# A recurrent stage in a kept order: swapped halves without state copies, gates split around tanh, sums and squares in place of bn_stats

## Chip, cores and metric

The kernel runs on one core of a Trainium2 chip. The metric is the device time of one execution in microseconds (us). The chip's engines are named as in the profile: PE is TensorE (PEld its weight loads), DVE is VectorE, ACT is ScalarE, POOL is GpSimd, and SP is SyncE, whose queue issues most of the DMAs.

## The reference, cut to what matters

Four layers work on x of shape (16, 32, 128, 128). Each adds to x a function of the group-normalised x (16 groups of two channels). The change lies in layer 0, a recurrence over the columns of a skewed image; the layers behind it are a quantised sum of absolute differences, a Hartley transform with mixing, and an encoder and decoder of convolutions.

```
xs[t] = W2 . skewed(norm(x))[:, :, :, t] + b2          # t = 0..127, (b, 4*32, h)
def step((pc, ph), xt):
    g  = xt + W1_prev . shift(ph) + W1_cur . ph + b1   # shift: by one row of h
    o, f, i = sigmoid(g[0:32]), sigmoid(g[32:64]), sigmoid(g[64:96])
    gg = tanh(g[96:128])
    nc = f * pc + i * gg
    nh = o * tanh(nc)
x1 = x + stack(nh over t)                              # then x1's mean and variance per group
```

All of it is float32. The mean and the variance of x1 are needed by the next layer before it can begin.

## The kernel before, in words

Partitions. The 512 rows of (batch, channel) form four groups g of 128 partitions, each of four batches by 32 channels. Stage 0 works on two chains c: chain 0 holds groups 0 and 1, chain 1 holds groups 2 and 3. A tile of a chain has 128 partitions and two column blocks, one per group.

Steps and chunks. The 128 time steps t are cut in NT = 16 chunks of T = 8. In chunk ch only the first n = min(8(ch+1)+2, 128) rows of h are computed, since the rows behind are equal to the last one; a tile of both groups has a width of 2n columns, 20 in the first chunk and 256 in the last. In each step the two chains take turns, so there are 256 chain steps, 16 in a chunk. At the end of a chunk the last column is spread to the rows that the next chunk adds (line 265).

The products. The weights are 64x64 blocks (two batches of 32 channels on the diagonal). A gate q needs three kinds of product: 0 with h, 1 with h shifted by one row, 2 with the normalised input xn. Each product is made of two matmuls on 64 partitions ("pair"), and each float32 matmul shows as two in the profile. For a gate with copy = 0 (F and G) input and output lie on the same half of the partitions. For a gate with copy = 1 (I and O) the weights of the other half of the array are used, so that four quadrants of the array work at once; these two gates read a copy of h with its halves swapped, the tile e (lines 258 to 260), and a copy of xn with its halves swapped, which SP makes by DMA after each normalise (line 177).

One chain step in the code (lines 223 to 265): sixteen products with h or e, eight products with xn for the next chain step, four gates on ACT (line 244: F, I, G, O, each reading a PSUM bank of its own), on DVE c*F (251), i*g (252) and their sum (253), tanh of c on ACT (255), h (256), and the two swapped copies into e (260).

Around the recurrence. `load(ch)` brings a chunk of xn and of the residual x (tile res) into SBUF. `normalise(ch, xn, g)` scales and shifts xn on ACT (line 174). `add` adds h to res on DVE (lines 185 and 188, the second for the rows beyond n), takes bn_stats of the result (189), and stores x1 (191). At the end bn_aggr (277) and norm_stats make the mean and the variance of x1.

The order. In stage 0 the order of the instructions on each engine is chosen by the scheduler of the framework. The function `keep_order(nc, tc, start)` makes every instruction since `start` follow the previous one of its engine in the order of the program; in the kernel before, only the stage behind (the differences, ACT and DVE bound) is kept that way. That stage and those after it are woven by a planner with costs of its own, which the change does not touch.

Of the kernel before, what the change touches and what calls it, by code (L numbers as in the profile page):

```python
# [100 lines left out]
def stage0(nc, tc, keep, cst, x, xs, w0, b1, b2, x1):  # L101
# [9 lines left out]
    PAIRS = ((F, I), (G, O))  # L111
    with ExitStack() as ctx:
# [33 lines left out]
        ex = [[sm.tile([128, 2, H + 1], F32, name=f"e_{c}_{i}") for i in range(2)] for c in range(2)]  # L146
        cs = [sm.tile([128, 2, H], F32, name=f"c_{c}") for c in range(2)]
        for c in range(2):
            nc.vector.memset(cs[c], 0.0)
            nc.vector.memset(hs[c][1][:, T - 1], 0.0)  # L150
            for i in range(2):
                nc.vector.memset(hs[c][i][:, :, :, 0], 0.0)
                nc.vector.memset(ex[c][i], 0.0)

        stat1 = sm.tile([128, NG, 32, 6], F32, name="stat1")
# [7 lines left out]
        def load(ch):  # L163
            steps = slice(T * ch * H, T * (ch + 1) * H)
            xn = [xp.tile([128, NG, T, H], F32, name=f"xn{i}") for i in range(2)]
            res = rp.tile([128, NG, T, H], F32, name="res")
            for g in range(NG):
                nc.sync.dma_start(flat(xn[0], g), bc_view(xs, g)[:, steps])
                nc.sync.dma_start(flat(res, g), bc_view(x, g)[:, steps])
            return xn, res  # L170

        def normalise(ch, xn, g):
            v = xn[0][:, g, :, : T * (ch + 1)]
            nc.scalar.activation(v, v, AF.Identity, bias=shift[:, g : g + 1], scale=r0[:, g : g + 1])
            for half in range(2):
                own, other = slice(64 * half, 64 * half + 64), slice(64 - 64 * half, 128 - 64 * half)
                nc.sync.dma_start(flat(xn[1], g)[own], flat(xn[0], g)[other])

        def add(ch, res, g, half):
# [4 lines left out]
            r = res[:, g, steps, :n]  # L184
            nc.vector.tensor_add(r, r, h[:, :, 1 : n + 1])
            if n < H:
                r = res[:, g, steps, n:]
                nc.vector.tensor_add(r, r, bcast(h[:, :, n], 2, H - n))
            nc.vector.bn_stats(stat1[:, g, 2 * ch + half, :], flat(res, g)[:, 512 * half : 512 * half + 512])
            if half:  # L190
                nc.sync.dma_start(bc_view(x1, g)[:, T * ch * H : T * (ch + 1) * H], flat(res, g))

# [5 lines left out]
        for g in range(NG):  # L198
            normalise(0, xn, g)

        with tc.tile_pool(name="s0_gps", bufs=1, space=PSUM) as gps:
            bank = [[gps.tile([128, 2, 256], F32, name=f"pg{c}_{q}") for q in range(4)] for c in range(2)]

            def product(c, kind, q, copy, pair, v, width):

                half = slice(64 * (pair ^ copy), 64 * (pair ^ copy) + 64)
                nc.tensor.matmul(  # L207
                    bank[c][q][64 * pair : 64 * pair + 64, :, :width],
                    wb[half, 4 * kind + KIND[q]].rearrange("p b o -> p (b o)"),
                    v[half],  # L210
                    start=kind == 2,
                    stop=kind == 1,
                    skip_group_check=True,
                )

            def inputs(c, t, xn):
                for gates in PAIRS:
                    for copy, q in enumerate(gates):
                        for pair in range(2):
                            v = xn[copy][:, 2 * c : 2 * c + 2, t % T, : t + 1]  # L220
                            product(c, 2, q, copy, pair, v, t + 1)

            inputs(0, 0, xn)
            for ch in range(NT):
                n = rows(ch)
                following = load(ch + 1) if ch + 1 < NT else None
                for j in range(T):
                    t = T * ch + j
                    for c in range(2):
                        h_in = (hs[c][ch % 2][:, j - 1] if j else hs[c][(ch - 1) % 2][:, T - 1], ex[c][t % 2])  # L230
                        h_out, cell = hs[c][ch % 2][:, j], cs[c][:, :, :n]
                        for gates in PAIRS:
                            for kind in range(2):
                                for copy, q in enumerate(gates):
                                    for pair in range(2):
                                        v = h_in[copy][:, :, 1 - kind : n + 1 - kind]
                                        product(c, kind, q, copy, pair, v, n)
                        if c == 0:
                            inputs(1, t, xn)
                        elif t + 1 < W:  # L240
                            inputs(0, t + 1, xn if j + 1 < T else following[0])
                        gt = gp.tile([128, 4, 2, H], F32, name=f"gt{c}")
                        for q in (F, I, G, O):
                            nc.scalar.activation(  # L244
                                gt[:, q, :, :n],
                                bank[c][q][:, :, :n],
                                AF.Tanh if q == G else AF.Sigmoid,
                                bias=bias[:, KIND[q] : KIND[q] + 1],
                            )
                        ig = gp.tile([128, 2, H], F32, name=f"ig{c}", bufs=1)  # L250
                        nc.vector.tensor_mul(cell, cell, gt[:, F, :, :n])
                        nc.vector.tensor_mul(ig[:, :, :n], gt[:, I, :, :n], gt[:, G, :, :n])
                        nc.vector.tensor_add(cell, cell, ig[:, :, :n])  # L253
                        th = gp.tile([128, 2, H], F32, name=f"th{c}")
                        nc.scalar.activation(th[:, :, :n], cell, AF.Tanh)  # L255
                        nc.vector.tensor_mul(h_out[:, :, 1 : n + 1], gt[:, O, :, :n], th[:, :, :n])  # L256
                        e_out = ex[c][(t + 1) % 2]
                        for half in range(2):
                            own, other = slice(64 * half, 64 * half + 64), slice(64 - 64 * half, 128 - 64 * half)
                            nc.vector.tensor_copy(e_out[own, :, 1 : n + 1], h_out[other, :, 1 : n + 1])  # L260
                        if j == T - 1 and n < H:

                            m = rows(ch + 1)
                            for v in (h_out[:, :, 1:], e_out[:, :, 1:], cs[c]):
                                nc.vector.tensor_copy(v[:, :, n:m], bcast(v[:, :, n - 1], 2, m - n))
                    if following and 2 <= j < 6:
                        normalise(ch + 1, following[0], j - 2)
                    if j >= T // 2:
                        add(ch, res, j - T // 2, 0)
                    elif ch:  # L270
                        add(ch - 1, previous, j, 1)
                previous = res
                if following:
                    xn, res = following
            for g in range(NG):
                add(NT - 1, previous, g, 1)
# [1702 lines left out]
```

## Time and profile before

| what | value |
|---|---|
| median of 3 runs | 7142.77 us (7139.5 to 7150.18) |
| the profiled execution, its own time | 7141.35 us |
| its span, first to last instruction | 7139.6 us |
| mean granted clock of TensorE | 0.907 |
| busy in the span: PE, DVE, ACT | 78%, 81%, 76% |
| first gate of stage 0; first h; last h | 96.8; 105.1; 841.4 us |
| ns_mean (statistics of x1 begin) | 846.9 us |

In the profile a row names a line of the kernel, the engine, the operation, the tile written and the tile read, the shapes and the count, then the busy time and the mean time of one. "Idle before" is the time for which the engine stood still just before these instructions, with what released it. The busy shares are means over stages that have different limits; those of the whole span say little about stage 0. In a timeline a row has the start, the duration, the engine and line, and instructions alike are merged in one row.

### The profile page before, as it was taken

The numbers are of one execution on the slowest core, as the hardware profiler recorded it, in microseconds if no ns is written. First come the engines' busy times: TensorE is split into PE (matmuls) and PEld (weight loads), VectorE is DVE, ScalarE is ACT, GpSimd is POOL, SyncE is SP. The second block draws the span as 40 slices with busy tenths as digits, with TensorE's granted clock in tenths as the row PEclk, the third lists the DMA queues.
The fourth block names the chain that finished last, engine by engine and source line by source line (L and its number), as shares of the span: only waits on it lengthen the run. The fifth ranks groups of instructions, "written<-read, shape, count | busy, mean of one in ns | idle before, by whom it ended". The sixth has DMA issues, their size and how long they took to land. (4 is left out here: it accounts for less than half of the span.)

```text
span 7139.6 us, 271100 instructions
## 1 busy us (share of the span) xinstructions
PE 5578.2 (78%) x127580; PEld 2940.1 (41%) x127580; DVE 5753.4 (81%) x7112; ACT 5452.3 (76%) x3099; POOL 81.9 (1%) x83
## 2 busy tenths in 40 slices
PE   4778667778876777999776787999886774698896
PEld 3666333333433333333333443333333343454564
DVE  7787689999998989999997999999998993134224
ACT  2555489999998989999998999999998991131222
POOL 0000000000000000000000001000000000000000
PEclk9899889999998999999888998999898996798997
DMA  8664211111123342221244243121243245252414
GB/s 312 225 211 147 83 62 58 60 59 39 56 88 108 121 107 87 62 78 37 70 121 114 96 135 112 52 76 50 66 106 120 68 133 166 80 173 73 98 40 99
DMA packets 372718, 722.55 MB, mean 101 GB/s; under 512 B 50896, under 2 KB 217296, under 8 KB 360720
## 3 DMA queue, kind: packets, MB, share of 16 engines
q1 hardware_dynamic: 364128, 670.79, 30.9%
q0 software_dynamic: 7040, 33.80, 1.4%
q8 instruction: 998, 16.35, 0.9%
q14 instruction: 120, 0.98, 0.0%
q10 hardware_dynamic: 432, 0.64, 0.0%
HBM read 507.28 MB, written 164.32 MB: 94 GB/s over the span
## 5 line engine op out<-in xcount | busy, mean ns | idle before, releaser
L705 ACT ACTIVATE d_act<-q,neg 128x8192 f16<-128x8192 f16 (+1 forms) x622 | 4402.5, 7149 | 182.1 <-PE acc L595 133.3
L708 DVE TENSOR_SCALAR d_dve<-q,qw 128x8192 f16<-128x8192 f16 (+1 forms) x1682 | 3877.5, 2361 | 168.0 <-PE acc L595 125.5
L595 PE MATMUL acc<-d_dve,sel 128*32 128x512 f16 x26912 | 1877.6, 403 | 507.3 <-DVE d_dve L708 441.5
L595 PEld LDWEIGHTS <-sel 128*32 128x32 f16 x36864 | 1022.7, 100 | 2203.4 <-issue 1547.7
L1670 PE MATMUL acc<-xp,wf 32*32 32x512 f32 x25600 | 1034.3, 616 | 44.0 <-issue 39.4
L595 PE MATMUL acc<-d_act,sel 128*32 128x512 f16 x9952 | 720.5, 411 | 376.1 <-ACT d_act L705 368.0
L1670 PEld LDWEIGHTS acc<-xp,wf 32*32 32x32 f32 x25600 | 420.5, 104 | 417.4 <-issue 329.8
L625 PE MATMUL acc<-q,zero 128*32 128x512 f16 x7088 | 510.1, 399 | 0.0
L1608 ACT ACTIVATE y<-pooled,b 32x128 f32<-32x128 f32 x488 | 195.0, 400 | 402.1 <-DVE pooled L1594 395.5
L207 PE MATMUL pg<-h,wb 64*64 64x20 f32 (+15 forms) x4096 | 397.6, 320 | 102.0 <-DVE h L256 60.7
L852 PE MATMUL acc<-y,u_conv 32*32 32x256 f32 (+1 forms) x9728 | 366.3, 474 | 76.5 <-issue 50.6
L244 ACT ACTIVATE gt<-pg,bias 128x20 f32<-128x20 f32 (+15 forms) x1024 | 314.9, 374 | 78.9 <-PE pg L207 71.7
L207 PE MATMUL pg<-e,wb 64*64 64x20 f32 (+15 forms) x4096 | 353.1, 315 | 18.2 <-DVE e L260 6.3
L1311 ACT ACTIVATE xp<-xp,shift,stats 128x1280 f32<-128x1280 f32 (+1 forms) x128 | 182.6, 1434 | 217.2 <-DMA xp<-x_d 193.6
L207 PEld LDWEIGHTS pg<-h,wb 64*64 64x64 f32 x4096 | 246.0, 153 | 137.5 <-DVE h L256 86.9
L625 PEld LDWEIGHTS <-zero 128*32 128x32 f16 x7088 | 215.0, 102 | 198.4 <-issue 44.7
L207 PE MATMUL pg<-xn,wb 64*64 64x28 f32 (+61 forms) x4096 | 283.6, 302 | 10.9 <-ACT gt L244 3.2
L207 PEld LDWEIGHTS pg<-e,wb 64*64 64x64 f32 x4096 | 250.1, 155 | 96.8 <-DVE e L260 67.6
L1352 PE MATMUL acc<-xp 32*64 32x204 f32 (+3 forms) x8576 | 242.3, 346 | 38.4 <-ACT xp L1317 28.6
L1799 DVE TENSOR_SCALAR s<-acc,l_ms,l_one 128x512 f32<-128x512 f32 x128 | 102.1, 820 | 207.1 <-PE acc L852 207.1
L255 ACT ACTIVATE th<-c 128x20 f32<-128x20 f32 (+15 forms) x256 | 81.3, 320 | 239.4 <-DVE c L253 238.0
L852 PEld LDWEIGHTS acc<-y,u_conv 32*32 32x32 f32 x9728 | 175.0, 112 | 196.8 <-issue 146.2
(215 smaller groups left out, 4070.5 us busy)
## 6 DMA issues: line engine op xcount, KB each, us to landing
xr<-x_d SPq DMA_DIRECT2D x192, 512.0 KB
xp<-x_d SPq DMA_DIRECT2D x112, 640.0 KB
q<-q_d SPq DMA_DIRECT2D x32, 2145.0 KB
x_d<-xr SPq DMA_DIRECT2D x128, 512.0 KB
x_in<-in_x_dram SPq DMA_DIRECT2D x16, 2048.0 KB
res<-in_x_dram SPq DMA_DIRECT2D x64, 512.0 KB
xn<-in_xs_dram SPq DMA_DIRECT2D x64, 512.0 KB
xn<-xn SPq DMA_DIRECT2D x128, 256.0 KB
```

The lines of the kernel that those rows point to most:

```text
L207: nc.tensor.matmul(bank[c][q][64 * pair : 64 * pair + 64, :, :width], wb[half, 4 * kind + KIND[q]].rearrange("p b o -> p (b o)"), v[half], ...
L244: nc.scalar.activation(gt[:, q, :, :n], bank[c][q][:, :, :n], AF.Tanh if q == G else AF.Sigmoid, bias=bias[:, KIND[q] : KIND[q] + 1],)
L595: self.nc.tensor.matmul(acc[k][32 * j : 32 * j + 32, :], self.sel16[:, i // 9, :], d[:, row : row + 4, c : c + W], start=first, stop=last,)
L625: self.nc.tensor.matmul(acc[k][32 * j : 32 * j + 32, :], self.zero, q[:, :4, :W], start=False, stop=False)
L705: nc.scalar.activation(dst, src, AF.Relu, bias=self.neg[:, i : i + 1])
L708: nc.vector.tensor_scalar(dst, src, self.qw[:, i : i + 1], 0.0, ALU.subtract, ALU.max)
L852: nc.tensor.matmul(acc[blk][32 * j : 32 * j + 32, o : o + rows * n], t[part, 4 * par + tap, :], src[part, top : top + rows, left : left + ...
L1311: nc.scalar.activation(v, v, AF.Identity, bias=self.shift3, scale=self.stats3[:, 1])
L1352: nc.tensor.matmul(gram[blk][j : j + width, at : at + n], xp[part, l, 2 + j : 2 + j + width], xp[part, rows, j : j + width + 4], start=sta ...
L1608: nc.scalar.activation(d, s, AF.Identity, bias=bj)
L1670: nc.tensor.matmul(acc[blk][32 * j : 32 * j + 32, :], tap_of("all", tap)[rows], xp[rows, 4 * j + kh : 4 * j + kh + 4, kw : kw + W], start= ...
L1799: nc.vector.tensor_scalar(s.rearrange("p r w b -> p b r w"), acc[blk].rearrange("p (b r w) -> p b r w", b=2, w=64), istd[:, blk : blk + 1] ...
```

## The change

- Gates I and G, in place of I and O, use the other half of the array (SWAPPED). They read the same h and xn as F and O, and their results come out on the swapped half of the partitions. The tile e, the copies into it, the second xn tile and its DMAs go.
- i*g is then made in two multiplies of 64 partitions that read the swapped half and write the own half.
- The chain step is written out in a fixed order, kept by `keep_order`: gates I and F, one piece of other ACT work (half a normalise, or a square), tanh of the chain step before, gates G and O. On DVE: one half of an add, h of the chain step before, c*F, i*g, c+i*g. The products run in the order I,F then G,O, and then the inputs of the next chain step.
- normalise works on four of the eight steps at a time.
- bn_stats and bn_aggr go. The add becomes a tensor_tensor_reduce that also sums its result; ACT squares the result less the mean of x (bias `away`) and sums the squares. Two reductions and four small operations make mean and variance from them.

```diff
-    PAIRS = ((F, I), (G, O))
+    SWAPPED = (I, G)
...
         def add(ch, res, g, half, part):
...
-            nc.vector.tensor_add(r, r, h[:, :, 1 : n + 1])
...
-            nc.vector.bn_stats(stat1[:, g, 2 * ch + half, :], flat(res, g)[:, 512 * half : 512 * half + 512])
+                nc.vector.tensor_tensor_reduce(
+                    r, r, v, 1.0, 0.0, ALU.add, ALU.add, accum_out=sums[:, g, ch, half, part : part + 1]
+                )
...
+        def square(ch, res, g, half):
+            nc.scalar.activation(
+                junk,
+                flat(res, g)[:, 512 * half : 512 * half + 512],
+                AF.Square,
+                bias=away[:, g : g + 1],
+                accum_out=squares[:, g, ch, half : half + 1],
+            )
...
+            def product(c, kind, q, v, width):
+                for pair in range(2):
+                    own = pair ^ (q in SWAPPED)
+                    half = slice(64 * own, 64 * own + 64)
+                    nc.tensor.matmul(
+                        bank[c][q][64 * pair : 64 * pair + 64, :, :width],
+                        wb[half, 4 * kind + KIND[q]].rearrange("p b o -> p (b o)"),
+                        v[half],
...
+            def state(c, ch, j, n, gt):
+                th = gp.tile([128, 2, H], F32, name=f"th{c}")
+                nc.scalar.activation(th[:, :, :n], cs[c][:, :, :n], AF.Tanh)
+                def write():
+                    h = hs[c][ch % 2][:, j]
+                    nc.vector.tensor_mul(h[:, :, 1 : n + 1], gt[:, O, :, :n], th[:, :, :n])
+                    if j == T - 1 and n < H:
+                        m = rows(ch + 1)
+                        for v in (h[:, :, 1:], cs[c]):
+                            nc.vector.tensor_copy(v[:, :, n:m], bcast(v[:, :, n - 1], 2, m - n))
+                return write
...
+                for s in range(2 * T):
+                    j, c = s // 2, s % 2
...
+                    for gates in ((I, F), (G, O)):
+                        for kind in range(2):
+                            for q in gates:
+                                product(c, kind, q, h_in[:, :, 1 - kind : n + 1 - kind], n)
+                    if c == 0:
+                        inputs(1, t, xn)
+                    elif t + 1 < W:
+                        inputs(0, t + 1, xn if j + 1 < T else following[0])
+                    gt = gp.tile([128, 4, 2, H], F32, name=f"gt{c}")
+                    gate(I)
+                    gate(F)
+                    if following and 3 <= s < 11:
+                        normalise(ch + 1, following[0], (s - 3) // 2, (s - 3) % 2)
+                    elif waiting:
+                        square(*waiting.pop(0))
+                    write = state(*before) if before else None
+                    if s >= T or ch:
+                        at = (ch, res, s // 2 - T // 2, 0) if s >= T else (ch - 1, previous, s // 2, 1)
+                        add(*at, s % 2)
+                        if s % 2:
+                            waiting.append(at)
+                    if write:
+                        write()
+                    gate(G)
+                    gate(O)
+                    nc.vector.tensor_mul(cell, cell, gt[:, F, :, :n])
+                    ig = gp.tile([128, 2, H], F32, name=f"ig{c}", bufs=1)
+                    for half in range(2):
+                        own, other = slice(64 * half, 64 * half + 64), slice(64 - 64 * half, 128 - 64 * half)
+                        nc.vector.tensor_mul(ig[own, :, :n], gt[other, I, :, :n], gt[other, G, :, :n])
+                    nc.vector.tensor_add(cell, cell, ig[:, :, :n])
+                    before = c, ch, j, n, gt
...
+            keep_order(nc, tc, start)
+            nc.vector.tensor_reduce(mv[:, :, 0], sums.rearrange("p g a b c -> p g (a b c)"), AX.X, ALU.add)
+            nc.vector.tensor_reduce(mv[:, :, 1], squares.rearrange("p g a b -> p g (a b)"), AX.X, ALU.add)
```

## The prediction

> **What bounds the kernel now.** I read the page first, then cut out the part that the change touches. The page gives one span and says nothing of stages:
>
> ```profile
> span 7139.6 us, 271100 instructions
> ```
>
> The recurrence runs from 96.8 us (first gate) to 841.4 us (last h), so 745 us of the 7139.6 can move. Everything behind it keeps its instructions and their order; it starts when the statistics of x1 are ready (ns_mean at 846.86 us) and moves with them. The groups of the window 100 to 845 us (line, engine, operation, tiles, count | busy us, mean ns | idle before it and its releasers):
>
> ```profile
> L244 ACT ACTIVATE gt<-pg,bias 128x20 f32<-128x20 f32 (+15 forms) x1022 | 314.4, 374 | 78.9 <-PE pg L207 71.7
> L260 DVE COPY e<-h 64x20 f32<-64x20 f32 (+15 forms) x512 | 117.2, 229 | 25.1 <-DVE h L256 0.5
> L189 DVE BATCH_NORM_STATS2 stat<-res 128x6 f32<-128x512 f32 x128 | 87.8, 686 | 0.7
> ```
>
> So 205 us of DVE go into state copies and bn_stats. Is DVE on the path? The waits of the same window (who waited for whom, us in total, times, longest):
>
> ```profile
> ACT th L255 <- DVE c L253: 238.0, 214, 5.3
> PEld pg L207 <- DVE h L256: 86.9, 110, 2.7
> DVE h L256 <- ACT th L255: 83.3, 188, 0.8
> ```
>
> ACT waits for DVE's cell in 214 of 256 steps, DVE for tanh in 188: the two hand one step to and fro. Timelines of one step at width 228 (columns of both batch groups together), ACT, then DVE, then PE:
>
> ```profile
> 717.11 0.39 ACT L255 ACTIVATE th<-c 128x228 f32<-128x228 f32 x1 [0.99 <-DVE c L253]
> 717.41 1.46 ACT L244 ACTIVATE gt<-pg,bias 128x228 f32<-128x228 f32 x4
> ```
> ```profile
> 717.54 0.40 DVE L256 TENSOR_TENSOR h<-gt,th 128x228 f32<-128x228 f32 x1 [0.52 <-ACT th L255]
> 718.04 0.56 DVE L260 COPY e<-h 64x228 f32<-64x228 f32 x2
> 718.63 0.40 DVE L251 TENSOR_TENSOR c<-c,gt 128x228 f32<-128x228 f32 x1
> 718.95 0.39 DVE L252 TENSOR_TENSOR ig<-gt 128x228 f32<-128x228 f32 x1
> 719.37 0.40 DVE L253 TENSOR_TENSOR c<-c,ig 128x228 f32<-128x228 f32 x1
> ```
> ```profile
> 718.90 0.36 PE L207 MATMUL pg<-e,wb 64*64 64x228 f32 x2
> ...
> 719.10 0.36 PE L207 MATMUL pg<-e,wb 64*64 64x228 f32 x2
> ...
> 719.29 0.36 PE L207 MATMUL pg<-e,wb 64*64 64x228 f32 x2
> ```
>
> One step is DVE's five pieces in a row plus the tanh that DVE waits for: 0.43 (tanh to h), 0.50, 0.60 (copies), 0.31, 0.42, 0.49 (sum to next tanh) = 2.75 us, the pace of the steady steps. PE needs 12 slots of 0.19 us (four quadrants at once): 2.3 us, no bound. The adds and bn_stats fall between chunks, where the pace is lost: at width 228 sixteen steps took 731.68 - 676.51 = 55.2 us, 3.45 each. From first h (105.13) to last (841.39): 736.3 / 255 = 2.89 us a step.
>
> **What the change makes of a step.** The kept order is, on ACT: I, F, one extra (half a normalise, or a square), tanh of the step before, G, O; on DVE: one add-with-sum, h of the step before, c*F, two halves of i*g, c+ig; on PE: I,F products (4 slots), G,O (4), inputs of the next step (4). The next PE step needs the h written in this one. So the loop becomes: tanh, h, I,F products, gates I and F, the extra, the next tanh. G, O and the cell update fall out of the loop, and the extra falls in. Its terms, from rows of before (W = width in columns):
> - tanh start to h start: 0.28 (W=52), 0.33 (116), 0.43 (228); h start to first matmul: 0.27, 0.34, 0.45.
> - I,F products to gate I: at 228 three slots 0.19, last matmul 0.36, first-use 0.05, and 0.06 from matmul end to gate (763.95 to 764.02 us): 1.04. At 116 (slot 0.10): 0.68. At 52 (slot 0.057): 0.50.
> - two gates: pitch 0.33 at 228 (1.46 us for four, last one 0.46), 0.24 at 116, 0.19 at 52: twice that.
> - the extra: a half normalise of N columns. The full one at N=512 starts 0.71 us before its follower, at N=256 0.49, so 0.28 + 0.00083 N. The square (512 columns, bias operand, summed) has no row. Lower end: the gates' pitch carried to 512, 0.57; upper: the normalise's 0.71 plus 0.1 for the sum, 0.8. I take 0.63: nearer the normalise without its second operand. 124 squares lie in the loop; the ends make -7 and +21 us.
> Sum: 1.01 + 0.00686 W + extra. By width, against the mean step of before:
>
> ```
> W       20    52    84    116   148   180   212   244   256
> before  2.62  2.52  2.42  2.55  2.75  3.07  3.34  3.56  3.5
> after   1.54  1.92  2.12  2.37  2.61  2.86  3.11  3.35  3.08
> ```
>
> (The first chunk has few extras, the last no normalise.) All sixteen widths, sixteen steps each: 648 us. The 15 chunk ends keep two of three boundary copies (0.17 us each, L265) ahead of a matmul: +7.5 us.
>
> **The clock, row against rule.** Between 120 and 125 us PE is busy 5.00 of 5.00 us, yet a weight load there takes 223 ns; at 345 us it takes 132 ns with PE busy only 3.54 of 5. The profile calls both granted clock 1.00. The Trainium skill ("TensorE: Matmul & The Clock Gate", Part 1) says some 4 us of sustained matmuls bring the full rate. By the rule the sum stays 655; by the row busy time is not enough at small widths, and the slow rate first ended near 205 us, at width 52, and came back in spells until about 300. I take the row: slots twice as long in the first five chunks, 0.28 to 0.33 us a step, 80 steps: +24 us, so 679 us for 256 steps, 676 for the 255 between first and last h.
>
> **DVE under it, and a rule against the change.** Added: one more multiply of 64 partitions (0.387 at 228) and a read of the accumulator in each add. The existing add-up of this kind shows the price (grouped by form):
>
> ```profile
> L1412 DVE CUSTOM_DVE_ANT_0 es_w<-acc,gm 128x420 f32<-128x420 f32 x80 | 47.5, 593 | 20.2 <-PE acc L1352 9.8 <-DMA gm<-in_gram_dram 7.2 <-DVE es_red L1412 0.5
> L1412 DVE DVE_READ_ACCUMULATOR2_ANT es_red<- 128x1 f32 x80 | 6.6, 82 | 0.0
> ```
>
> At 420 columns 593 ns, like a plain add (594 at 424), plus 82. Removed: two copies (0.56) and bn_stats (0.686 each, 128 times). In the trace independent DVE operations overlap by about 0.08 us (c*F at 718.63, 0.40 long, ig at 718.95). The skill ("VectorE: DVE Perf Modes", Two Vector instructions with no wait between them) says that one which starts in another quadrant than its forerunner is held until all earlier ones end. The halves of i*g cross partitions, so both are held, and the sum after them. With overlap DVE's step at 228, long add included, is 0.31 + 0.31 + 0.31 + 0.42 + 0.31 + 0.63 + 0.08 = 2.4 us, by the rule 2.7. Both are under the loop's 3.23, so I cost it at nothing; the cover is 0.5 us a step, and beyond it every 0.1 us costs 26 us. A late DVE would hold h, and behind it PE.
>
> **Queues.** SP loses 128 swap issues (0.46 to 2.15 us each, waiting for ACT) and 32 MB of traffic; PE waited 1.5 us for them once. The loads of xn no longer stand behind them. Eight loads of 512 KB need some 10 us at the 375 GB/s of a chunk's start; the first normalise stands at step 3, and SP issues the loads once the older xn is free, one step before the chunk: lead about 8 us for the first piece. An ACT wait there would stall tanh and both gates behind it; I cost it at nothing.
> Start: PE need not wait for the swapped input (matmuls on xn at 102.99 us after 1.51 us). Chain 1 still needs groups 2 and 3 (98.75 us), so I put the first h at 101.3 instead of 105.13. End: four adds (0.70 apart), one square, two reductions, four small operations: 5.9 us from last h to ns_mean, 5.5 before.
>
> **The sum.** 101.3 + 676.4 + 5.9 = 783.6 against 846.9: -63 us. Profiled execution: 7141.35, its span 7139.6, so 1.75 us lie around it. 7141.35 - 63 = 7078; the median of the runs is 1.4 above that execution: 7080.
>
> **Rivals.**
> - *The extra on ACT, or DVE, sits in the loop for more than I allow* (chance 0.18). Square at 0.8, held DVE operations that use up the cover at narrow widths (at W=36 the cover is only 0.2 us): 0.1 to 0.15 us a step, 25 to 38 us back: about 7112. For: four engines hand over in one loop and none of the small latencies has slack. Against: every latency is taken from the same tiles.
> - *The early chunks run at full clock* (0.10): -24 us, 7056. For: the products no longer wait in pairs, so matmuls come denser. Against: the row at 120 us.
> - *PE stays at half rate: slower* (0.07). PE now works 0.8 to 2.6 us of each step and pauses up to 1.2. If the gate never opens, 12 slots of W/600 us bind above width 170: 5.1 us at 256. Widths 100 to 256 cost 159 us more, so about 7239. It decides if half rate lasts beyond width 196 (its excess up to there is 63 us). For: before drops to 0.50 at 220 us after a boundary. Against: it ran at 1.00 from 340 to 430 us with PE waiting in every step, and the boundary stalls go. The skill's rule (same section) puts the fall only behind gaps of over 3 us.
> - *Nothing comes of it* (0.05): the copies were hidden and the serial loop of two chains eats the rest; within 15 us of 7143. Against: copies are 0.60 of 2.75 in the very chain above.
> The likeliest, at 0.60: 7080, own range 7055 to 7105.
>
> **Numbers.** About 0.2%, 14 us, is what a measurement of this kernel can tell from no change. Faster 0.88 (the likeliest, the first two rivals), same 0.04 (of the last rival), slower 0.08 (half rate, and 0.01 of the last). The range 7045 to 7125 leaves out the half-rate case, no change and the ends of the rest.
>
> **What would show it.** Right: ACT idle before gate I "<- PE pg", not before tanh; h about 3.2 us apart at width 228 without double gaps at chunk ends; the statistics near 784 us; later stages unchanged. Wrong: DVE never idle in the stage, or h waiting after tanh has ended (DVE binds); weight loads of 223 ns beyond width 116 (clock); ACT waiting on the xn load.

## The result, and the profile after

| | before | after |
|---|---|---|
| median of 5 runs | 7142.77 us (7126.25 to 7150.18) | 7116.38 us (7102.01 to 7124.78) |
| profiled execution, its span | 7141.35, 7139.6 us | 7102.01, 7100.1 us |
| first h, last h | 105.1, 841.4 us | 103.2, 802.4 us |
| ns_mean (statistics of x1 begin) | 846.9 us | 807.6 us |
| statistics copied to the next layer | 850.8 us | 811.5 us |

The ratio is 0.9957, with a 95% interval from 0.9942 to 0.9971: the kernel became faster, by 26 us between the medians where 63 were forecast. In the profiled executions stage 0 gave back 39.3 us (850.8 - 811.5), and what lies behind it kept its length (7139.6 - 850.8 = 6288.8 us before, 7100.1 - 811.5 = 6288.6 after). So the main question is why stage 0 gave 39 us and not 63; why the medians differ by 13 us less than stage 0 comes at the end.

The span of the page, and then the waits of the window 95 to 900 us (who waited for whom, us in total, times, longest), one row of the kernel before and five of the changed kernel:

```profile
span 7100.1 us, 270757 instructions
```
```profile
POOL qt L528 <- DVE stats L97: 850.8, 1, 850.8
```
```profile
POOL qt L567 <- DVE stats L97: 811.5, 1, 811.5
PEld pg L221 <- DVE h L249: 233.1, 219, 1.4
DVE h L249 <- ACT th L245: 230.3, 253, 4.0
ACT gt L235 <- PE pg L221: 196.0, 255, 1.7
PE pg L221 <- DVE h L249: 174.5, 212, 1.3
```

The POOL rows are a tile that is cleared once the statistics are there: their release dates the end of stage 0. The other rows name the new loop: PE waits for h, ACT's gates wait for PE, h waits for tanh. Each of them occurs in 212 to 255 of the 256 chain steps, and the wait of tanh for the cell (238 us before) is gone (1.5 us, once). It is the loop that the prediction drew. The groups of stage 0, window 95 to 815 us (count | busy us, mean ns | idle before):

```profile
L235 ACT ACTIVATE gt<-pg,bias 128x20 f32<-128x20 f32 (+15 forms) x1024 | 329.8, 376 | 196.0 <-PE pg L221 196.0
...
L196 ACT ACTIVATE junk<-res,away 128x512 f32<-128x512 f32 x128 | 92.0, 719 | 0.6 <-DVE sums L189 0.5
L196 ACT ACTIVATION_READ_ACCUMULATOR junk<-res,away 128x1 f32 x128 | 25.3, 197 | 0.0
```
```profile
L297 DVE TENSOR_TENSOR ig<-gt 64x20 f32<-64x20 f32 (+15 forms) x512 | 153.5, 300 | 6.9
L189 DVE CUSTOM_DVE_ANT_1 res<-res,h 128x40 f32<-128x40 f32 (+15 forms) x248 | 105.9, 428 | 0.0
```

The rows of copies and bn_stats (205 us of DVE) have no successor; DVE got 256 more multiplies of i*g, and ACT got the squares, each followed by a row that had no counterpart before: a read of the accumulator, 197 ns. One step at width 228:

```profile
644.76 0.79 ACT L235 ACTIVATE gt<-pg,bias 128x228 f32<-128x228 f32 x2 [1.03 <-PE pg L221]
645.44 0.72 ACT L196 ACTIVATE junk<-res,away 128x512 f32<-128x512 f32 x1
646.05 0.20 ACT L196 ACTIVATION_READ_ACCUMULATOR junk<-res,away 128x1 f32 x1
646.14 0.39 ACT L245 ACTIVATE th<-c 128x228 f32<-128x228 f32 x1
646.57 0.40 DVE L249 TENSOR_TENSOR h<-gt,th 128x228 f32<-128x228 f32 x1 [1.11 <-ACT th L245]
647.01 1.77 PE L221 MATMUL pg<-h,wb 64*64 64x228 f32 x32 [0.80 <-DVE h L249]
648.05 0.80 ACT L235 ACTIVATE gt<-pg,bias 128x228 f32<-128x228 f32 x2 [0.83 <-PE pg L221]
```

Read the starts: gate I to square 0.68, square to tanh 0.70 (of which the accumulator's read holds the last 0.09), tanh to h 0.43, h to the first matmul 0.44, from there to the next gate I 1.04. The step is 3.29 us. A half normalise stands in the other steps of the chunk; its pitch is 0.68. Tanh, h, products and gates take 2.6 us of this; the rest is the piece of ACT work that has nothing to do with the recurrence.

### The profile page after: what moved, and what is told of

It is laid out like the page before. It is cut to its first block, busy times and chain, and to the rows that moved or that the text cites. A ratio compares the mean times of both kernels' runs of the same rounds, so it can differ in the third digit from the quotient of the medians.

```text
span 7100.1 us, 270757 instructions
## 1 busy us (share of the span) xinstructions
PE 5456.6 (77%) x127580; PEld 2865.6 (40%) x127580; DVE 5635.0 (79%) x6946; ACT 5541.3 (78%) x3419; POOL 82.1 (1%) x83
## 3 DMA queue, kind: packets, MB, share of 16 engines
q1 hardware_dynamic: 353888, 637.22, 29.2%
## 5 line engine op out<-in xcount | busy, mean ns | idle before, releaser
L1709 PE MATMUL acc<-xp,wf 32*32 32x512 f32 x25600 | 1017.8, 616 | 38.4 <-issue 34.7
L221 PE MATMUL pg<-h,wb 64*64 64x20 f32 (+15 forms) x8192 | 355.3, 319 | 204.9 <-DVE h L249 174.5
L235 ACT ACTIVATE gt<-pg,bias 128x20 f32<-128x20 f32 (+15 forms) x1024 | 329.8, 376 | 196.0 <-PE pg L221 196.0
L221 PEld LDWEIGHTS pg<-h,wb 64*64 64x64 f32 x8192 | 263.3, 161 | 291.5 <-DVE h L249 233.1
L249 DVE TENSOR_TENSOR h<-gt,th 128x20 f32<-128x20 f32 (+15 forms) x256 | 78.1, 305 | 230.4 <-ACT th L245 230.3
L1811 ACT ACTIVATE xr<-xr,l_ms 128x1024 f32<-128x1024 f32 x64 | 69.9, 1140 | 219.9 <-DVE xr L1801 219.9
L1391 PEld LDWEIGHTS acc<-xp 32*64 32x64 f32 (+1 forms) x8576 | 170.0, 136 | 125.1 <-issue 90.1
L221 PE MATMUL pg<-xn,wb 64*64 64x2 f32 (+63 forms) x4096 | 186.7, 303 | 9.1 <-ACT xn L177 7.3
```

What stands on the lines that cost most here:

```text
L221: nc.tensor.matmul(bank[c][q][64 * pair : 64 * pair + 64, :, :width], wb[half, 4 * kind + KIND[q]].rearrange("p b o -> p (b o)"), v[half], ...
L235: nc.scalar.activation(gt[:, q, :, :n], bank[c][q][:, :, :n], AF.Tanh if q == G else AF.Sigmoid, bias=bias[:, KIND[q] : KIND[q] + 1],)
L1391: nc.tensor.matmul(gram[blk][j : j + width, at : at + n], xp[part, l, 2 + j : 2 + j + width], xp[part, rows, j : j + width + 4], start=sta ...
L1709: nc.tensor.matmul(acc[blk][32 * j : 32 * j + 32, :], tap_of("all", tap)[rows], xp[rows, 4 * j + kh : 4 * j + kh + 4, kw : kw + W], start= ...
```

## The experiments

All changes are against the changed kernel unless it is said otherwise; each ratio is to the kernel before, run in the same round. "Statistics" is the end of stage 0, read as above. The pace is the mean distance between two writes of h from the start of a chunk to that of the next, named by the chunk's width. Theory A is that of the prediction: the loop is tanh, h, I,F products, gates I and F, and the extra; whatever stands in that loop costs its own pitch.

**The extra behind gate O.** The half normalise or square stays, but ACT does it after all four gates, where it waits for the next products anyway.

```diff
                     gate(I)
                     gate(F)
-                    if following and 3 <= s < 11:
-                        normalise(...)
-                    elif waiting:
-                        square(*waiting.pop(0))
                     write = state(*before) if before else None
 ...
                     gate(G)
                     gate(O)
+                    if following and 3 <= s < 11:
+                        normalise(...)
+                    elif waiting:
+                        square(*waiting.pop(0))
```

> The changed kernel with one edit: the extra piece of ACT work (half a normalise or a square) stands behind gate O instead of between gate F and tanh. Theory A (the loop is tanh, h, I and F products, gates I and F, the extra, the next tanh; the extra is in the loop at full price): each of the some 244 steps with an extra gets shorter by 0.55 to 0.75 us, the pace at width 228 goes from 3.33 to about 2.65, at 256 to 2.8 in every step; stage 0 ends about 130 to 150 us earlier (statistics near 670 us), time 6965 to 6990. Rival B (DVE or ACT is nearly full and binds as soon as the extra leaves the loop): DVE's row of operations at width 228 is 2.5 us long, so the pace would stay at 2.9 or more and the time at 7060 or more.

Measured: 6951.68 us (4 runs), ratio 0.9744 (0.9727 to 0.9762); statistics at 676.2 us, 135 us earlier than with the extra in the loop; pace 2.66 instead of 3.35 at width 228. Waits and a step at 228 of this kernel:

```profile
DVE h L249 <- ACT th L245: 89.4, 185, 4.0
ACT gt L235 <- PE pg L221: 58.9, 124, 3.4
PE pg L221 <- issue: 21.3, 15, 3.6
```
```profile
570.93 0.73 ACT L196 ACTIVATE junk<-res,away 128x512 f32<-128x512 f32 x1
571.54 0.21 ACT L196 ACTIVATION_READ_ACCUMULATOR junk<-res,away 128x1 f32 x1
571.89 0.79 ACT L235 ACTIVATE gt<-pg,bias 128x228 f32<-128x228 f32 x2
572.58 0.39 ACT L245 ACTIVATE th<-c 128x228 f32<-128x228 f32 x1
573.00 0.40 DVE L249 TENSOR_TENSOR h<-gt,th 128x228 f32<-128x228 f32 x1
573.45 1.77 PE L221 MATMUL pg<-h,wb 64*64 64x228 f32 x32
574.49 0.80 ACT L235 ACTIVATE gt<-pg,bias 128x228 f32<-128x228 f32 x2
```

The idle time of ACT before gate I fell from 196 to 59 us: the square now fills it. The loop is tanh to h 0.42, to the matmul 0.45, to the gates 1.04, to the next tanh 0.69, 2.60 in all, and the extra appears in it no more. Theory A is confirmed, a little beyond its numbers (6965 to 6990 us were expected), and this version beats both kernels. It has a new loss, nearly all of it in the chunks up to width 132: in 15 places, 21 us in all, PE stands still while the profile names nothing that it waits for (third row; 2 us in the changed kernel). What that is stays open.

**No kept order.** The scheduler places the same instructions.

```diff
-            keep_order(nc, tc, start)
```

> The changed kernel without keep_order in stage 0: the same instructions, ordered by the framework's scheduler. Theory A (the copies' removal is the gain, the kept order adds the even pace and the extra in the loop): the extras slide into ACT's idle time but adds and sums bunch again at chunk ends; time between 7040 and 7110. Rival (the kept order is what gained): 7130 or slower than before.

Measured: 7086.87 us, ratio 0.9936 (0.9922 to 0.9951); statistics at 809.5 us, 2 us before those of the kept order. The paces differ: 2.00 against 2.35 at width 68, but 3.55 against 3.35 at 228. The time lies in the range of Theory A. Against this very order the scheduler does as well; the gain of the change is not that of fixing an order.

**Adds and bn_stats back, no squares.** The half normalises stay in the loop, the ACT slots of the squares stay empty, and bn_aggr makes the statistics at the end.

```diff
-                nc.vector.tensor_tensor_reduce(
-                    r, r, v, 1.0, 0.0, ALU.add, ALU.add, accum_out=sums[...]
-                )
+                nc.vector.tensor_add(r, r, v)
+            if part:
+                nc.vector.bn_stats(stat1[:, g, 2 * ch + half, :], flat(res, g)[...])
 ...
-                    elif waiting:
-                        square(*waiting.pop(0))
```

> The changed kernel with plain adds and bn_stats on DVE again, in the kept order, and no squares on ACT. Theory A (a square costs its whole 0.7 to 0.75 us in the loop, DVE has cover): 124 steps get 0.7 shorter, less some 0.1 us where bn_stats fills DVE; stage 0 ends 70 to 90 us earlier, time 7025 to 7050; so sums and squares in place of bn_stats would be a loss where they stand. Rival B (DVE binds): bn_stats bring 0.69 us into every other step, which takes away what the squares gave; 7100 to 7120.

Measured: 7025.32 us, ratio 0.9846 (0.9828 to 0.9864); statistics at 752.1 us. Where they stand, sums and squares cost 59 us of stage 0 (811.5 - 752.1); Theory A had 70 to 90. DVE has room for the bn_stats in many steps, not in all: h waits for tanh in 159 steps, where it was 253. In 88 of the others h starts straight behind a bn_stats, as will be seen in the last experiment; at width 116 a step without half normalise takes 2.37 us with a bn_stats and 1.87 without.

```profile
DVE h L249 <- ACT th L245: 87.4, 159, 4.0
```

**Swapped copies back.** Gates I and O read copies again, with the DMAs of the second xn tile; i*g is one multiply, and the products of F stand ahead of those of I. All else is as changed, in the kept order.

```diff
-    SWAPPED = (I, G)
+    SWAPPED = (I, O)
 ...
+                    e = ex[c][(T * ch + j + 1) % 2]
+                    for side in range(2):
+                        ...
+                        nc.vector.tensor_copy(e[own, :, 1 : n + 1], h[other, :, 1 : n + 1])
 ...
-                    for half in range(2):
-                        ...
-                        nc.vector.tensor_mul(ig[own, :, :n], gt[other, I, :, :n], gt[other, G, :, :n])
+                    nc.vector.tensor_mul(ig[:, :, :n], gt[:, I, :, :n], gt[:, G, :, :n])
```

> The changed kernel with I and O on swapped copies again (the state copies into e after each h, the second xn by DMA, one multiply for i*g), everything else as changed, kept order included. Theory A (copies stand in the loop): the products of I wait 0.4 to 0.65 us longer for e, so the pace at width 228 goes from 3.33 to 3.9, and stage 0 takes 110 to 150 us more; time 7225 to 7265, slower than the kernel before. Rival (copies are hidden beside the F products): within 20 us of 7116.

Measured: 7257.4 us, ratio 1.017 (1.0151 to 1.0189); statistics at 966.6 us. In this loop the copies, with what comes along with them, are worth 155 us, 0.61 us a step; some 6 us of it lie ahead of the first h (109.1 against 103.2 us). That is more than the copies' 229 ns a piece, two a step (0.46): their rows are not the whole price. PE waits for e after it has waited for h, as the third row has it. One step at width 212, below the waits, shows where the price lies: the first matmuls on h start 0.43 us behind h (749.21 us), the copies 0.48 behind it; they take 0.54, and the first matmuls on e start 0.06 after them. So PE can go on only 0.65 us after its first matmul of the step, and the pace at this width is 0.66 us longer than in the changed kernel (3.88 against 3.22).

```profile
ACT gt L241 <- PE pg L227: 352.1, 256, 4.4
DVE h L255 <- ACT th L251: 308.5, 256, 3.8
...
PEld pg L227 <- DVE e L259: 77.2, 222, 0.7
```
```profile
749.64 0.58 PE L227 MATMUL pg<-h,wb 64*64 64x212 f32 x4 [0.89 <-DVE h L255]
749.69 0.54 DVE L259 COPY e<-h 64x212 f32<-64x212 f32 x2
750.29 0.40 PE L227 MATMUL pg<-e,wb 64*64 64x212 f32 x2
```

**The changed kernel again.** Run in the same round as the next three.

> The changed kernel once more, unedited, for a second profile and more timed runs. Theory A: stage 0 ends near 811 us again (last copy of the statistics) and everything behind it takes the same 6289 us; differences of the whole time between runs come from the clock: spells of half rate at widths up to some 116 in stage 0 (each step there costs 0.3 to 0.4 us more) and from the later stages. Then the ratio to the kernel before is 0.994 to 0.997. Rival: the one profiled execution was an exception, and stage 0 ends beyond 825 us in most.

Measured: 7099.26 us (7090.23 to 7102.96), ratio 0.995 (0.9937 to 0.9962); statistics at 812.4 us. The medians of this round differ by 34 us, nearer to the 39 of the stage.

**More work for PE in the narrow chunks.** The products with xn are made twice in the first seven chunks (the second pass starts the sums anew, so nothing else changes), to see whether the half clock there goes and what that is worth.

```diff
+                    for again in range(2 if ch < 7 else 1):
                         if c == 0:
                             inputs(1, t, xn)
                         elif t + 1 < W:
                             inputs(0, t + 1, ...)
```

> The changed kernel with the input products of each chain step made twice in the first seven chunks (widths 20 to 116), which writes the same values again: 16 matmul passes more a step, behind the recurrent products, only to keep PE busier. Theory A (half clock in the early chunks stretches the I,F products, and density brings the full clock earlier): weight loads of 132 ns from width 52 or so on, the pace at widths 68 to 116 falls by 0.2 to 0.35 us a step where it was at half rate, in all 10 to 25 us less than the changed kernel. Rival B: the rate depends on something else or the added matmuls stand in the way of the next step's products: same time or up to 20 us more.

Measured: 7101.47 us, ratio 0.9959 (0.9944 to 0.9974); statistics at 815.7 us, 4 us later than in the changed kernel where Theory A had 10 to 25 earlier. First three stretches of the changed kernel, then two of this one (window: length, busy us of PE, PEld, DVE, ACT, POOL with counts, granted clock, DMA share, GB/s), the first of them the chunk of width 100 in the changed kernel (in the other it begins 9 us later):

```profile
283.00:325.00 42.00, 29.21 (x772) 25.41 (x768) 25.61 (x117) 29.39 (x108) 0.00 (x0) 0.70 0.43 165
325.00:366.00 41.00, 27.14 (x768) 23.40 (x768) 26.87 (x116) 29.57 (x102) 0.00 (x0) 0.85 0.40 151
366.00:408.00 42.00, 25.10 (x768) 21.34 (x768) 28.23 (x116) 31.81 (x106) 0.00 (x0) 1.00 0.41 154
```
```profile
283.00:325.00 42.00, 27.81 (x1088) 24.52 (x1088) 27.18 (x124) 31.51 (x116) 0.00 (x0) 0.96 0.47 167
325.00:366.00 41.00, 28.88 (x1028) 25.21 (x1032) 27.05 (x120) 30.34 (x105) 0.00 (x0) 1.00 0.45 162
```

With 1088 matmuls in place of 772 PE is busy for less time, at a clock of 0.96 instead of 0.70. This stretch alone does not show that the density did it, for the clock in it differs from run to run: 0.74 in the second run of the changed kernel, 0.94 in the run without the sum (below), which makes no product twice. The stretches to both sides speak for it: from 325 us on 1.00 here, 0.83 to 0.88 in those three runs; and from 200 to 281 us the weight loads of the products with h take 161 ns in the mean here, 195 to 212 ns there (132 at the full clock). The pace at widths 84, 100 and 116 improved from 2.40, 2.60, 2.61 to 2.32, 2.41, 2.55: 5.3 us in these three chunks. The doubled products cost 9 us in the four narrowest ones, so there was nothing to win. The half clock was real, and lasted longer than forecast; what could be got back of it is small.

**Tanh ahead of gate I**, on top of the kernel with the extra behind gate O.

```diff
+                    write = state(*before) if before else None
                     gate(I)
                     gate(F)
-                    write = state(*before) if before else None
```

> The version with the extra behind gate O, and with the tanh of the step before moved ahead of gate I. Theory A (tanh then waits for its cell alone, so the loop over PE spans two steps and DVE's row of 2.1 to 2.5 us or PE's 2.3 us sets the pace): pace at width 228 from 2.66 to about 2.45, narrow widths unchanged since ACT is full there; 15 to 40 us less than that version. Rival B (ACT stands still at tanh until the cell is there, and gates I and F behind it come late): slower by 20 us or more, DVE waiting for tanh in every step as in the kernel before.

Measured: 6981.18 us, ratio 0.9787 (0.977 to 0.9804); statistics at 698.5 us, 22 us later than with tanh behind gate F; the pace at width 228 is 2.81 where Theory A had 2.45. The cell now waits for a gate in 207 steps, and tanh for the cell in 188, each of which happens once in that kernel:

```profile
DVE c L293 <- ACT gt L235: 73.0, 207, 3.8
ACT th L245 <- DVE c L298: 62.8, 188, 1.1
```

Tanh needs the cell, which DVE makes from gates I, F and G of the step before; asked for sooner, tanh is the instruction that ACT waits at, and gates I and F come behind it: they wait for PE only 15 times. This is Rival B, though not in all: h waits for tanh in 83 steps, not in every one.

**Half normalises on POOL**, on top of the last one.

```diff
-            nc.scalar.activation(v, v, AF.Identity, bias=shift[...], scale=r0[...])
+            nc.gpsimd.tensor_scalar(v, v, r0[...], shift[...], ALU.mult, ALU.add)
```

> As the last one, with the half normalises on POOL in place of ACT. Theory A (ACT is the fullest engine at widths up to some 150): 0.28 to 0.7 us of ACT work leave half of the steps, the pace at widths 36 to 132 falls by 0.1 to 0.2 us; 10 to 30 us less than with normalises on ACT. Rival B (POOL takes several us for a piece, or its traffic slows DVE): xn comes late at chunk starts or DVE's operations get longer; same or slower.

Measured: 7003.88 us, ratio 0.9816 (0.9803 to 0.983); the last h at 706.7 us, 17 us later than with ACT doing it. POOL needs longer than ACT for one (738 against 623 ns in the mean), but has time. The group, and then one step's sum c+i*g without and one with a half normalise on POOL at its side:

```profile
L177 POOL TENSOR_SCALAR xn<-xn,is_y,shift 128x32 f32<-128x32 f32 (+15 forms) x128 | 93.4, 738 | 526.3 <-DMA xn<-in_xs_dram 275.6 <-PE pg L221 155.8 <-DVE shift L126 94.9
```
```profile
606.64 0.40 DVE L298 TENSOR_TENSOR c<-c,ig 128x228 f32<-128x228 f32 x1
609.08 2.53 POOL L177 TENSOR_SCALAR xn<-xn,is_y,shift 128x512 f32<-128x512 f32 x2 [36.52 <-DMA xn<-in_xs_dram]
609.42 0.85 DVE L298 TENSOR_TENSOR c<-c,ig 128x228 f32<-128x228 f32 x1
```

The same sum takes 0.40 us alone and 0.85 us beside POOL. Of the 1280 operations that make h and the cell, 65 took over 1.3 times the median of their kind and width; every one of these overlaps with a half normalise on POOL, and none of the 1074 that do not overlap took so long. Against the kernel with tanh ahead of gate I the means grew from 304 to 317 ns (h), 305 to 316 (c*F), 300 to 310 (i*g, two a step) and 305 to 324 (the sum): 63 ns a step, 16 us over 256 steps. So the slower DVE is nearly the whole of the 17 us, as Rival B had it.

**Squares without their sum.** The square keeps its place in the loop; the sum of its result is left out (so the variance is made from a constant).

```diff
+        nc.vector.memset(squares, 256.0)
 ...
                 AF.Square,
                 bias=away[:, g : g + 1],
-                accum_out=squares[:, g, ch, half : half + 1],
```

> The changed kernel with the squares left in their place, but without the sum of their result (so the variance of x1 is left out: it is made from a constant). Theory A: my term for the square was too small because of the sum; the summing square is followed by an ACTIVATION_READ_ACCUMULATOR of 197 ns, and tanh starts 0.70 to 0.75 us behind the square's start. Without the sum the square should cost 0.55 to 0.60, as the lower end of my estimate, so 124 squares give back 0.12 to 0.20 us each, 15 to 25 us: the last copy of the statistics 787 to 797 us (811.5 before this edit), the time 7072 to 7088 us. Rival B: the read lies beside the pipeline and costs nothing; square and tanh are then still 0.68 us or more apart and the statistics stay within 5 us of 811.5; the time stays at 7095 to 7110.

Measured: 7090.95 us, ratio 0.9938 (0.9919 to 0.9958); statistics at 799.2 us, 12.3 us earlier than in the changed kernel. That is between the two expectations and nearer to A's. Not all of it is the sum's: at width 100 the pace fell by 0.23 us, most of which is the clock (above). Where the clock is full, at widths 148 to 244, it fell by 0.047 us (0.029 at 228), which is 0.09 us for each square, one in two steps; over 124 squares that is 12 us, so the clock's gains and losses nearly cancel. The step shows it exactly:

```profile
632.52 0.79 ACT L235 ACTIVATE gt<-pg,bias 128x228 f32<-128x228 f32 x2 [1.06 <-PE pg L221]
633.21 0.72 ACT L197 ACTIVATE junk<-res,away 128x512 f32<-128x512 f32 x1
633.82 0.37 ACT L245 ACTIVATE th<-c 128x212 f32<-128x212 f32 x1
```

From square to tanh 0.61 instead of 0.70 or 0.71, and the square's own duration is unchanged (719 ns).

**Half normalises behind gate O, with bn_stats.** Is bn_stats still the better choice once ACT's extra is out of the loop? Against the kernel with bn_stats back:

```diff
-                    if following and 3 <= s < 11:
-                        normalise(...)
 ...
                     gate(O)
+                    if following and 3 <= s < 11:
+                        normalise(...)
```

> The half normalises behind gate O, and plain adds with bn_stats on DVE in place of sums and squares; the rest as in the changed kernel. It asks whether sums and squares are worth anything once ACT's extra work is out of the loop. Theory A: yes. DVE then carries per step, at 228 columns, 2.4 to 2.7 us of cell work and add plus half a bn_stats (0.34 us), 2.75 to 3.05 in all, against a loop of about 2.65; from some 130 columns on DVE binds, 0.1 to 0.3 us a step over nine chunks, 15 to 40 us: statistics 690 to 715 us, time 6965 to 6995, slower than the kernel with the extra behind gate O (6952). Rival B: DVE still hides it; statistics within 8 us of 676 or earlier, time 6940 to 6958.

Measured: 6990.67 us, ratio 0.9801 (0.978 to 0.9821); statistics at 712.0 us. Sums and squares, a loss of 59 us inside the loop, are a gain of 36 us outside it (712.0 - 676.2). The expected size came out, the expected shape did not: the excess over the kernel with the extra behind gate O is 0.07 to 0.23 us a step at the widths up to 212 and only 0.04 to 0.07 from 228 on. DVE is not full over two steps together; but one bn_stats stands ahead of h in every second step, and there DVE has no idle time, here at width 116:

```profile
306.65 0.48 DVE L189 TENSOR_TENSOR res<-res,h 128x312 f32<-128x312 f32 x1
307.16 0.69 DVE L191 BATCH_NORM_STATS2 stat<-res 128x6 f32<-128x512 f32 x1
307.77 0.26 DVE L249 TENSOR_TENSOR h<-gt,th 128x116 f32<-128x116 f32 x1
...
309.03 0.36 DVE L189 TENSOR_TENSOR res<-res,h 128x200 f32<-128x200 f32 x1
309.63 0.28 DVE L249 TENSOR_TENSOR h<-gt,th 128x116 f32<-128x116 f32 x1 [0.24 <-ACT th L245]
```

The steps with it are 2.40 us, those without 1.87; in the kernel with the extra behind gate O they are 1.82 to 1.89, but for two at the chunk's end (2.11 and 2.13) and two of 2.90 and 2.91, in which PE stood still as said above. Of the 36 us some 4 lie behind the last h, where four bn_aggr of 1.01 us stand.

Stage 0 by its end, then:

| kernel (kept order but for the first) | statistics, us |
|---|---|
| before | 850.8 |
| copies back, sums and squares and normalise in the loop | 966.6 |
| changed kernel: no copies, sums and squares and normalise in the loop | 811.5 |
| no copies, bn_stats, normalise in the loop | 752.1 |
| no copies, bn_stats, normalise behind gate O | 712.0 |
| no copies, sums and squares and normalise behind gate O | 676.2 |

## Why the prediction was right in its direction and wrong in its size

- **The mechanism: right.** The loop is the one that was drawn. Its terms at 228 came out at 0.43, 0.44, 1.04 and 0.68 (0.66 forecast for two gates), and a half normalise at 0.68, which is what 0.28 + 0.00083 N gives for 480 columns. Taking the extra out of the loop takes its pitch out of the step.
- **The failed step: the terms of the sum under "What the change makes of a step" and "The clock, row against rule".** The way from first h to last was put at 676.4 us and took 699.2. The 22.8 us lie as follows, by comparing the forecast pace of each width with the measured one (the prediction's line "1.01 + 0.00686 W + extra" comes to some 644 us for the sixteen widths where it has 648, since its table stands 0.11 and 0.05 us above the line at widths 20 and 52; against the line the miss is 4 us larger):
  - *The square*, put at 0.63, is 0.70 to 0.71. 124 times 0.08 us is 10 us. The operation alone was sized well (0.61 without the sum); "plus 0.1 for the sum" had gone into the upper end and not into the value taken. The run without the sum gave back 0.09 us a square. This term is shown.
  - *The half clock* was ended after the fifth chunk. It went on into widths 100 and 116, whose paces were 0.32 and 0.20 us above the forecast where their wider neighbours are 0.09 above it: about 5.7 us. Weight loads of 223 ns came in spells until 364 us. The reading "until about 300" of the kernel before was short, too: between 325 and 340 us its weight loads still took 165 to 169 ns in the mean. The run with more PE work gained as much (5.3 us, though at widths 84 to 116). In widths 52 to 84, where it had been allowed for, the forecast held within some 0.05 us: to go by the row and not by the rule was right, it was only not carried far enough.
  - *The two narrowest chunks* were some 0.15 and 0.17 us a step slower than the sum, 5 us; no run isolated why.
  - *The rest*, some 2 us on balance, is small terms of both signs: the products to gate I take 1.03 to 1.04 in eight steps of the chunk at 228 and 1.09 to 1.10 in the other eight, most of which carry a half normalise; two gates take 0.02 more than forecast. These were seen and not explained.
- **The start** came at 103.2 instead of 101.3 us: "Chain 1 still needs groups 2 and 3" was the right dependency, but the piece of xn that it waited for came late, for a reason that no run isolated. In the changed kernel:

```profile
101.10 0.71 ACT L177 ACTIVATE xn<-xn,shift,is_y 128x32 f32<-128x32 f32 x2 [1.71 <-DMA xn<-in_xs_dram]
```

- **The tail** took 5.1 us where 5.9 were forecast. So 22.8 + 1.9 - 0.8 = 23.9, which is the 63 that were forecast less the 39.3 that stage 0 gave.
- **DVE under it: right.** It costs nothing in the changed kernel: h waits for tanh in 253 steps. The two multiplies of i*g are 0.80 us long at 228 and do not overlap, and the sum follows 0.83 after the first; the first starts 0.40 after c*F, which is 0.39 long, where the undivided i*g of before started 0.32 after a c*F of 0.40. That is as the Trainium skill has it ("VectorE: DVE Perf Modes", Two Vector instructions with no wait between them), and without effect on the time here.
- **Queues: right.** ACT waits for a load of xn at the start alone, twice, 2.3 us in all.
- **Rivals.** The one with the extra on ACT in the loop for more than allowed (7112) came true in part: the square did take more, DVE did not bind. That the first median lies 4 us from its number is luck, since the clock, the narrowest chunks, the start and the spread behind stage 0 make up most of the distance from 7080. The early chunks did not run at full clock: until 224 us nine in ten weight loads took some 223 ns. Half rate for good did not come either: the clock is 1.00 from 366 us on. That nothing would come of it is refuted by stage 0 (39 us) and by the copies put back (155 us).
- **The median against the stage.** The profiled pair differs by 39.3 us, the medians by 26 in the first round and by 34 in the second. The code behind stage 0 is the same in these kernels; yet after the statistics the end came between 6274 us later (no kept order; adds and bn_stats back) and 6293 (no sum), with 6279 for the extra behind gate O, 6289 for the changed kernel and 6287 for it again. A difference of 10 to 20 us between two times is therefore not to be put down to stage 0, and the 13 us between the stage's 39 and the first median's 26 are of that size; no run shows more of their cause.

What was missed at large is not in the account of 24 us. The prediction counted the extra as a cost of the loop and took the order as given; the same order, with four lines moved behind gate O, was 135 us faster in stage 0. That is over three times the gain of the whole change, and nearly the 155 us that the copies are worth in this order.

## What to carry to other kernels

Once a loop is known as a chain with terms, each instruction in it that the chain doesn't need is a term that can be moved: put it behind the last instruction that somebody waits for, where the engine waits anyway. Whether an operation is worth moving from one engine to another depends on this place more than on its duration: sums and squares lost 59 us ahead of tanh and gained 36 behind the gates. An output that is summed on the way counts as two instructions, and the value taken for it should include the second.

## What the runs showed of the hardware

- An ACTIVATE that also sums is followed by an ACTIVATION_READ_ACCUMULATOR of 197 ns; it overlaps the square by 0.11 us, so it adds 0.09 to 0.10 us to the pitch, not 0.20 (square to tanh 0.70 with it, 0.61 without).
- On DVE the summing add (428 ns in the mean over all widths) costs no more than the plain add with bn_stats back (427), plus 82 to 83 ns for the read of its accumulator.
- DVE operations beside a half normalise on POOL can take twice as long: a sum of 128x228 took 0.85 us instead of 0.40, and all 65 long ones of 1280 overlapped with POOL.
- More matmuls can take less PE time: 1088 in 27.8 us of busy time at a granted clock of 0.96, against 772 in 29.2 us at 0.70. That the denser stream brought the clock is likely from the stretches beside it, but the same stretch was granted 0.94 in a run without added matmuls.
